# Unread products placed in TensorE's expected stands, in a kernel whose instruction order is planned

## The chip, the cores and the metric

The kernel runs on one core of one Trainium2 chip. The metric is the device time of one execution in microseconds (us); smaller is better. Several executions are measured and the median counts. One execution is also recorded by the hardware profiler, and every reading below is from that one.

## What is computed

Eight sequences `x` of 512 tokens and 256 features go through two layers with residual sums, all in fp32:

```python
x = x + 0.5 * _L0_ffn_ref(_layernorm(x, axis=-1), L0_ffn_w_gate, L0_ffn_w_up, L0_ffn_w_down)
x = x + _L0_attn_ref(_layernorm(x, axis=-1), L0_attn_Wv, ..., L0_attn_Wo)
x = x + 0.5 * _L0_ffn_ref(_layernorm(x, axis=-1), L0_ffn_w_gate, L0_ffn_w_up, L0_ffn_w_down)
x = x + 0.5 * _L1_ffn_ref(_layernorm(x, axis=-1), L1_ffn_gamma_x, ..., L1_ffn_w2)
x = x + _L1_attn_ref(_layernorm(x, axis=-1), L1_attn_wq, ..., L1_attn_bo)
x = x + 0.5 * _L1_ffn_ref(_layernorm(x, axis=-1), L1_ffn_gamma_x, ..., L1_ffn_w2)
```

`_L0_ffn_ref` is a gated FFN of width 704 whose operands are rounded to FP4 in blocks of 16 (so the activations are rounded at run time). `_L0_attn_ref` is a retention layer with decay 0.99. `_L1_ffn_ref` is a soft mixture: 1,024 slots share one expert of width 1,024, with softmax weights over experts on the way in and over slots on the way out. `_L1_attn_ref` is causal attention of 16 heads with LoRA weights.

## The kernel before

The work of a sequence `b` is a row of stages: FFN, retention, FFN and `dispatch` of the mixture (the list `front`, line 1481), then attention and a second `dispatch` (`back`, line 1491). Each `dispatch` is followed by `experts` (line 1055), so there are 16 expert units. Three lanes (`front`, `back`, `experts`, line 1502) each walk through their own list, so that a product of one lane can stand between those of another. A stage is a Python generator that yields ahead of each step which PSUM banks the step takes and which results it needs.

Nothing is ordered by a fixed loop. `drive` (line 1432) chooses the next step by the planned clocks that `Meter` keeps: every instruction of every engine goes through `Meter.emit` (line 139), which estimates when it begins (`begins`, line 125: the latest of its engine's clock, of its inputs' writing and of the last use of its output, plus a hop of 0.12 us between engines) and what it costs (`cost`, line 196), moves that engine's clock and issues it. A step is ready when its needs lie within 0.3 us of TensorE's planned clock; among ready lanes the one that has had least of TensorE goes first. VectorE's small steps (rounding to FP4, normalising, softmax transposes) lie in chains that `fill` and `put_off` put where VectorE is expected to wait. The engines then run their own instructions strictly in that order.

The planner also keeps a model of TensorE's clock (`slow`, line 178). Planned time is cut into stretches of 3.413 us; a stretch with less than 5% of work is followed by half speed, one with more than 90% by full speed, and a stretch between leaves the speed as it is. All of TensorE's instructions count as work there, transposes too.

```python
            if self.worked < 0.05 * self.STRETCH:
                self.full = False
            elif self.worked > 0.9 * self.STRETCH:
                self.full = True
```

Names used below: `gu_f` is the FFN's up and gate product, `dn_f` its down product; `tr_f`, `tr_r` and `tr_m` are transposes of normalised rows ahead of FFN, retention and mixture, `hTp_f` those of the FFN's hidden rows, `nm_m` those of the largest logits; `k_r` and `q_r` are retention's key and query products; `lt_m`, `sl_m`, `h_e`, `p_e` and `mo_e` are the mixture's logits, slots, expert layers and output; `st_a` and `s_a` are attention scores. `y_ffn` is an input row tile, normalised and then rounded in place, `scale_*` and `rec_*` the 16 or 44 block scales of such a tile, `h_f` the hidden rows. `ident` and `identb` (lines 364 to 368) are identity matrices in fp32 and bf16, there for the transposes.

Of the kernel before, what the change touches and what calls it, by code (L numbers as in the profile page):

```python
# [20 lines left out]
FP = mybir.dt.float32  # L21
BF = mybir.dt.bfloat16
# [47 lines left out]
class Meter:  # L70
# [10 lines left out]
    STRETCH = 3.413  # L81
    HOLE = 0.3

    def __init__(self, nc):
        self._nc = nc
        self.at = dict.fromkeys(("PE", "DVE", "ACT", "POOL", "SP"), 0.0)
        self._written, self._used = {}, {}
        self._table, self._mode = None, None
        self.end, self.last = 0.0, None
        self.moved = 0.0  # L90

        self.far = set()

        self.stretch, self.worked, self.full = self.STRETCH, 0.0, False

        self.banks = set()

        self.holds = {"DVE": [], "POOL": []}

        self.kept, self.fill = None, None  # L100
        self.tensor = _Engine(self, "PE", nc.tensor)
        self.vector = _Engine(self, "DVE", nc.vector)
        self.scalar = _Engine(self, "ACT", nc.scalar)
        self.gpsimd = _Engine(self, "POOL", nc.gpsimd)
        self.sync = _Engine(self, "SP", nc.sync)
# [33 lines left out]
    def emit(self, engine, op, call, args, kwargs):  # L139
        aps = [x for x in (*args, *kwargs.values()) if isinstance(x, bass.AP)]  # L140
        if engine == "DVE" and self.fill:

            while self.begins(engine, aps) > self.at[engine] + self.HOLE and self.fill():
                pass
        at, cost = self.begins(engine, aps), self.cost(engine, op, args, kwargs, aps)
        if self.shares(engine, op, aps):

            other = self.holds["POOL" if engine == "DVE" else "DVE"]
            for a, b in sorted(other):
                if a < at + cost and at < b:  # L150
                    at = b
            other[:] = [x for x in other if x[1] > at - 20.0]
            self.holds[engine].append((at, at + cost))
        cost *= self.slow(at, cost) if engine == "PE" else 1.0
        at += cost
        self.at[engine] = self.end = at
        self.last = engine
        if engine == "SP":

            runs = int(np.prod(aps[1].shape[:-1])) if aps[1].ap[-1][0] == 1 else int(np.prod(aps[1].shape))  # L160
            bytes_ = int(np.prod(aps[0].shape)) * 4
            self.moved = max(self.moved, at) + max(bytes_ / self.BYTES, runs * self.RUN)
            self.end = at = self.moved + self.LANDS
        for k in self._pieces(aps[0]):
            self._written[k] = (engine, at)
        for x in aps:
            for k in self._pieces(x):
                self._used[k] = (engine, at)
            self._used[x.tensor.name] = at
        call(*args, **kwargs)  # L170

    def shares(self, engine, op, aps):
        if engine == "DVE":
            ins = sum(x.tensor.name not in self.banks for x in aps[1:])
            return ins > 1 or (op == "tensor_scalar" and self.banks.isdisjoint(x.tensor.name for x in aps))
        return engine == "POOL" and len(aps) > 1
# [104 lines left out]
def macaron(ctx: ExitStack, tc: tile.TileContext, a: dict, out: bass.AP):  # L281
    nc = Meter(tc.nc)
# [81 lines left out]
    ident = const.tile([P, P], FP, tag="ident", name="ident")  # L364
    make_identity(tc.nc, ident)

    identb = const.tile([P, P], BF, tag="identb", name="identb")
    nc.vector.tensor_copy(identb, ident)

    causalb = const.tile([P, 2, P], BF, tag="causalb", name="causalb")  # L370
    causalT = const.tile([P, P], FP, tag="causalT", name="causalT")
# [9 lines left out]
    for u in range(2):  # L381
        t = const.tile([P, NT, P], FP, tag=f"nmx{u}", name=f"nmx{u}")
# [1049 lines left out]
    def drive(until=lambda: False):  # L1432
        while not until():
# [19 lines left out]
            if ready:  # L1453
                emit(min(ready, key=lambda lane: lane.spent))
                continue
# [9 lines left out]
            if found and not (able and first <= nc.at["DVE"]):  # L1465
                go(*found)
            else:
                assert able, [(lane.name, lane.banks, lane.needs) for lane in live]
                emit(min(able, key=lambda lane: when[lane.name]))
# [94 lines left out]
```

## Time and profile before

| | |
|---|---|
| Time, median of 3 executions | 2965.66 us (2959.52 to 2970.26) |
| Profiled execution | 2961.62 us, of which the span from first to last instruction is 2959.7 us |
| TensorE (PE) busy | 2812.0 us, 95% of the span |
| VectorE (DVE), ScalarE (ACT), GpSimd (POOL) busy | 1651.6, 1174.8 and 128.1 us |
| Mean granted TensorE clock | 0.984 |
| PE busy in the first 330 us | 248.6 us, clock 0.89 |
| PE busy from 330 us to 2959 us | 2563.4 of 2629 us |

How to read it: the profile lists for each engine the busy time, and for each product a record of its beginning and modelled end, which overlap a little where products follow one another. "PEclk" is the share of TensorE's full clock that the chip granted. "Idle before" is the time an engine stood ahead of an instruction, with the instruction that released it. All operations are issued from one line of `Meter.emit`, so groups are told apart by the tiles' names. An fp32 product in the code appears as two matmul records.

### The profile page before, as it was taken

Reading aid. Unit: us, or ns where it says so; the run is one execution under the profiler, and the core shown is the slowest. Engines: PE = TensorE matmul, PEld = TensorE weight load, DVE = VectorE, ACT = ScalarE, POOL = GpSimd, SP = SyncE. Lnnn points to the kernel's source line nnn. Section 1 sums busy time; section 2 is a strip of 40 time slices with the busy share of each in tenths; the row PEclk is TensorE's granted clock in tenths of the full one; section 3 lists DMA queues with packets and bytes.
Section 4 is the critical chain, followed back from the end, with each engine's and each line's share of the span. In section 5 each row is a group of like instructions: output and inputs, shape, how many; then the busy total and the mean of one; then the engine's idle time right before and its main releaser. Section 6 shows DMA issues by size and latency. Waiting matters only on the chain.

```text
span 2959.7 us, 35020 instructions
## 1 busy us (share of the span) xinstructions
PE 2812.0 (95%) x13550; PEld 1946.7 (66%) x13550; DVE 1651.6 (56%) x4023; ACT 1174.8 (40%) x1587; POOL 128.1 (4%) x232
## 2 busy tenths in 40 slices
PE   4887999999999999999999999999899999999999
PEld 3554777657676577666766667666577666676668
DVE  7676755566565564655647456555565645436340
ACT  3333443434435343343525425254253443443321
POOL 1000000000000000000000000000000000000000
PEclk8988999999999999999999999999999999999999
DMA  3001101020200220002200031000220012000120
GB/s 118 1 0 35 40 24 45 1 75 1 68 1 1 82 64 5 1 1 82 68 1 1 1 114 36 1 1 1 82 68 1 1 43 79 22 1 20 56 75 8
DMA packets 71335, 98.13 MB, mean 33 GB/s; under 512 B 9472, under 2 KB 56320, under 8 KB 71168
## 3 DMA queue, kind: packets, MB, share of 16 engines
q1 hardware_dynamic: 71168, 95.88, 10.8%
q8 instruction: 107, 1.75, 0.2%
q14 instruction: 60, 0.49, 0.1%
HBM read 58.01 MB, written 37.85 MB: 32 GB/s over the span
## 4 chain that ended last, share of the span: by engine, by line
PE 87%; DVE 6%; ACT 4%; issue 1%; DMA 1%; SPq 1%; POOL 0%; ACTq 0%; DVEq 0%; POOLq 0%
PE p_e L170 14%; PE h_e L170 14%; PE gu_f L170 10%; PE lt_m L170 8%; PE sl_m L170 7%; PE mo_e L170 7%; PE dn_f L170 6%; PE s_a L170 4%; PE st_a L170 3%; PE c_a L170 2%; PE qk_a L170 2%; ACT L170 1%; PE hTp_f L170 1%; PE a_r L170 1%; PE y_r L170 1%; PE k_r L170 1%
## 5 line engine op out<-in xcount | busy, mean ns | idle before, releaser
L170 PE MATMUL h_e<-slT_m,w1g 128*128 128x256 f32 x2048 | 464.9, 381 | 4.2 <-DVE lg_m L170 2.4
L170 PE MATMUL p_e<-w,hid_e 128*128 128x256 f32 x2048 | 456.1, 381 | 3.4 <-ACT hid_e L170 2.0
L170 PEld LDWEIGHTS p_e<-w,hid_e 128*128 128x128 f32 x2048 | 386.3, 190 | 70.6 <-issue 13.3
L170 PEld LDWEIGHTS h_e<-slT_m,w1g 128*128 128x128 f32 x2048 | 382.3, 190 | 74.6 <-issue 11.2
L170 ACT ACT_TABLE_LOAD x274 | 351.5, 1283 | 109.0 <-DVE st_a L170 41.3
L170 PE MATMUL gu_f<-w_in,y_ffn 128*128 128x352 f32 x1024 | 333.8, 478 | 13.3 <-ACT y_ffn L170 11.8
L170 PEld LDWEIGHTS gu_f<-w_in,y_ffn 128*128 128x128 f32 x1024 | 198.7, 197 | 131.3 <-issue 19.4
L170 DVE TENSOR_REDUCE nmx<-s_a 128x2 f32<-128x256 f32 (+3 forms) x256 | 195.9, 818 | 126.3 <-PE s_a L170 126.1
L170 ACT ACTIVATE pT_a<-st_a 128x1024 f32<-128x1024 f32 (+1 forms) x192 | 159.0, 878 | 217.9 <-DVE st_a L170 205.1
L170 PE MATMUL lt_m<-yT_m,seT 128*128 128x512 f32 x512 | 235.5, 607 | 4.1 <-ACT yT_m L170 3.6
L170 ACT ACTIVATE hid_e<-h_e 128x1024 f32<-128x1024 f32 x128 | 130.8, 1023 | 268.5 <-PE h_e L170 268.1
L170 PE MATMUL mo_e<-proc_e,lg_m 128*128 128x257 f32 x1024 | 233.3, 381 | 2.9 <-DVE x L170 1.7
L170 PE MATMUL sl_m<-ed_m,y_dis 128*128 128x512 f32 x512 | 227.1, 594 | 3.9 <-DVE lg_m L170 3.3
L170 PEld LDWEIGHTS mo_e<-proc_e,lg_m 128*128 128x128 f32 x1024 | 190.7, 190 | 39.5 <-issue 4.9
L170 ACT COPY proc_e<-p_e 128x512 f32<-128x512 f32 x64 | 37.5, 586 | 391.9 <-PE p_e L170 391.9
L170 DVE TENSOR_SCALAR_CACHE_REDUCE lg_m<-lt_m 128x512 f32<-128x512 f32 x128 | 84.8, 682 | 173.3 <-PE lt_m L170 173.3
L170 PE MATMUL dn_f<-w_dn,hT_f 128*128 128x256 f32 x768 | 177.3, 383 | 0.0
L170 PEld LDWEIGHTS sl_m<-ed_m,y_dis 128*128 128x128 f32 x512 | 95.9, 190 | 114.9 <-issue 106.7
L170 PEld LDWEIGHTS lt_m<-yT_m,seT 128*128 128x128 f32 x512 | 96.2, 194 | 114.4 <-issue 101.3
L170 DVE TENSOR_TENSOR h_f<-h_f,gu_f 128x352 f32<-128x352 f32 x128 | 66.4, 519 | 177.8 <-ACT h_f L170 177.1
L170 PEld LDWEIGHTS dn_f<-w_dn,hT_f 128*128 128x128 f32 x768 | 143.1, 192 | 23.0 <-issue 4.2
L170 DVE TENSOR_TENSOR st_a<-st_a,causalT 128x256 f32<-128x256 f32 x256 | 100.9, 428 | 100.4 <-PE st_a L170 97.7
(197 smaller groups left out, 3246.3 us busy)
## 6 DMA issues: line engine op xcount, KB each, us to landing
d_ed_m<-ed_m SPq DMA_DIRECT2D x256, 128.0 KB
ed_m<-d_ed_m SPq DMA_DIRECT2D x64, 512.0 KB
rb_m<-row_rb_m SPq DMA_DIRECT2D x32, 256.0 KB
x<-in_L_attn_x SPq DMA_DIRECT2D x8, 512.0 KB
tm_m<-row_nm_m SPq DMA_DIRECT2D x16, 256.0 KB
out<-x SPq DMA_DIRECT2D x8, 512.0 KB
row_rb_m<-z_rb_m SPq DMA_DIRECT2D x128, 0.5 KB
w1g<-in_L_ffn_w SPq DMA_DIRECT2D x1, 1024.0 KB
```

What stands on the lines that cost most here:

```text
L170: call(*args, **kwargs)
```

## The change

`Meter.emit` gets one more step ahead of each TensorE instruction. If the planner expects TensorE to stand for more than `PACE` = 2.2 us ahead of a transpose or the first product of a sum (full height of 128 rows), it looks at which engine writes the awaited input last. From that engine's last 61 outputs (VectorE or ScalarE only, not PSUM) it takes those that are still the latest content of their tile, are two-dimensional with 128 rows and at least 16 contiguous columns, and are expected during the stand, at least 0.5 us ahead of its end. At steps of at most 2.2 us it emits a product of an identity with such an output, of up to 128 columns in fp32 or 512 in bf16 (two of them if it has under 128 columns), into the bank that the awaited product is going to overwrite. Nobody reads the result. These products go through `emit` as well: the planner charges them to TensorE's clock and counts them as work in `slow`.

```diff
+    PACE = 2.2
...
+        self.wrote = {"DVE": [], "ACT": []}
+        self.idents = {}
...
             while self.begins(engine, aps) > self.at[engine] + self.HOLE and self.fill():
                 pass
+        if engine == "PE" and self.idents:
+            self.keep_pace(op, aps, kwargs)
         at, cost = self.begins(engine, aps), self.cost(engine, op, args, kwargs, aps)
...
         for k in self._pieces(aps[0]):
             self._written[k] = (engine, at)
+        if engine in self.wrote and aps[0].tensor.name not in self.banks:
+            self.wrote[engine] = self.wrote[engine][-60:] + [(at, aps[0])]
...
+    def keep_pace(self, op, aps, kwargs):
+
+
+        begin, to = self.begins("PE", aps), aps[0]
+        if begin - self.at["PE"] <= self.PACE or to.shape[0] < 128 or len(to.shape) != 2:
+            return
+        if op != "transpose" and not kwargs.get("start"):
+            return
+        last = [(t + self.HOP, who) for x in aps[1:] for who, t in [self._written.get(k, ("PE", 0.0)) for k in self._pieces(x)]]
+        who = max(last)[1]
+        bank = max((self._used.get(k, ("PE", 0.0))[1] for k in self._pieces(to)), default=0.0) + self.HOP
+        found = []
+        for t, x in self.wrote.get(who, ()):
+            whole = all(self._written.get(k) == (who, t) for k in self._pieces(x))
+            plain = len(x.shape) == 2 and x.shape[0] == 128 and x.shape[1] >= 16 and x.ap[-1][0] == 1
+            if whole and plain and x.dtype in self.idents:
+                found.append((t + self.HOP, x))
+        while begin - self.at["PE"] > self.PACE:
+            now = self.at["PE"]
+            later = [f for f in found if f[0] > max(now + 0.3, bank) and f[0] < begin - 0.5]
+            if not later:
+                break
+            within = [f for f in later if f[0] <= now + self.PACE]
+            x = max(within, key=lambda f: f[0])[1] if within else min(later, key=lambda f: f[0])[1]
+            n = min(x.shape[1], to.shape[1], 512 if x.dtype == BF else 128)
+            for _ in range(1 if n >= 128 else 2):
+                kw = dict(start=True, stop=True)
+                self.run_on("PE", "matmul", (to[:, :n], self.idents[x.dtype], x[:, :n]), kw)
+
+    def run_on(self, engine, op, args, kwargs):
+        idents, self.idents = self.idents, {}
+        self.emit(engine, op, getattr(self._nc.tensor, op), args, kwargs)
+        self.idents = idents
...
     identb = const.tile([P, P], BF, tag="identb", name="identb")
     nc.vector.tensor_copy(identb, ident)
+    nc.idents = {FP: ident, BF: identb}
```

## The prediction, made before the changed kernel was run

> **What bounds the kernel now.** I read the page first: the busy times and the row of granted clocks.
>
> ```profile
> span 2959.7 us, 35020 instructions
> ...
> PE 2812.0 (95%) x13550; PEld 1946.7 (66%) x13550; DVE 1651.6 (56%) x4023; ACT 1174.8 (40%) x1587; POOL 128.1 (4%) x232
> ...
> PEclk8988999999999999999999999999999999999999
> ```
>
> TensorE is the bound. It stands 147.7 us in all (2959.7 - 2812.0), of which the first 330 us hold 81 (330 - 248.6). There the clock is 0.89. Second, the waits of PE, longest total first (total, times, longest):
>
> ```profile
> PE tr_f L170 <- DVE scale_h_f L170: 17.7, 2, 13.9
> PE gut L170 <- DMA Wk<-in_L_attn_Wk: 13.7, 1, 13.7
> PE tr_m L170 <- DVE y_dis L170: 11.9, 4, 3.8
> PE gu_f L170 <- ACT y_ffn L170: 11.8, 14, 3.3
> PE tr_f L170 <- DVE y_ffn L170: 11.3, 2, 6.8
> ```
>
> Few waits are long. Third, the busy time by stretches, cut at 46.95 us + k x 3.413 us. With these cuts every row shows a clock of exactly 1.00 or 0.50, so the clock changes on a fixed grid of 3.41 us (columns: PE, PEld, DVE, ACT, POOL busy, then PEclk):
>
> ```profile
> 67.43:70.84 3.41, 0.56 (x2) 0.00 (x0) 1.18 (x6) 0.00 (x0) 2.94 (x2) 1.00 0.00 0
> 70.84:74.25 3.41, 2.78 (x9) 2.01 (x10) 3.23 (x7) 3.35 (x9) 0.00 (x0) 0.50 0.00 0
> 77.67:81.08 3.41, 2.33 (x14) 1.48 (x13) 2.16 (x5) 2.29 (x5) 0.00 (x0) 1.00 0.00 0
> 81.08:84.49 3.41, 3.41 (x13) 2.24 (x12) 2.39 (x8) 1.14 (x2) 0.00 (x0) 1.00 0.00 0
> ...
> 279.05:282.47 3.42, 0.51 (x2) 0.00 (x0) 2.39 (x6) 3.37 (x7) 0.00 (x0) 1.00 0.00 0
> 282.47:285.88 3.41, 0.00 (x0) 0.00 (x0) 2.74 (x9) 3.40 (x7) 0.00 (x0) 0.50 0.02 5
> ...
> 2869.75:2873.16 3.41, 1.58 (x4) 0.87 (x5) 2.91 (x3) 1.51 (x2) 0.00 (x0) 1.00 0.95 356
> 2873.16:2876.57 3.41, 3.41 (x9) 1.52 (x8) 1.72 (x2) 3.23 (x4) 0.00 (x0) 1.00 0.90 327
> ```
>
> Each pair is a thinly used stretch and the next one. Products (not transposes) for 0.56 us (16%) or 0.51 us (15%) did not keep the clock; 1.58 us (46%) did, and so did the stretch from 77.67 us, with 0.86 us of products and the rest transposes. Fourth, the timeline of PE, for what a lowered clock costs:
>
> ```profile
> 159.08 0.66 PE L170 MATMUL tr_f<-ident,y_ffn 128*128 128x128 f32 x2 [6.75 <-DVE y_ffn L170]
> 160.24 8.04 PE L170 MATMUL gu_f<-w_in,y_ffn 128*128 128x352 f32 x16 [0.51 <-ACT y_ffn L170]
> ...
> 170.16 5.00 PE L170 MATMUL gu_f<-w_in,y_ffn 128*128 128x352 f32 x16 [1.66 <-ACT y_ffn L170]
> ```
>
> The same 16 records take 8.04 us after a stand of 6.75 us and 5.00 us otherwise.
>
> **What the clock costs.** From the stretches and the timeline there are eleven lowered periods ahead of the end. The excess of each is the row at half clock minus the same work elsewhere at full clock. Preceded by one stand over 2.2 us: from 53.8 us (`dnt`, `lora` and half a `gu_f`, about 6 us), 70.8 (`se` 2.52 - 1.04, `gu_f` 4.46 - 2.53: 3.4), 91.3 (`gu_f` 6.69 - 5.00: 1.7), 156.2 (8.04 - 5.00: 3.0), 282.5 (7.41 - 5.00: 2.4), 756.9 (`dn_f` 4.13 - 2.76, `hTp_f` 1.20 - 0.82: 1.8). Sum 18.3 us; call these reachable. Not reachable: from 118.6 (`k_r` 6.32 - 3.60: 2.7), 197.1 (`k_r` 6.65 - 3.60: 3.1), 248.3 (`lt_m` 9.99 - 7.03: 3.0), 989.1 (1.8) and 2084.7 (`lt_m` 5.62 - 3.60 and transposes: 2.6), 13.2 us. Ahead of these the stretch holds several stands of 0.4 to 2.2 us between transposes; none passes `PACE`, and the planner counts the transposes as work. So even a perfect change leaves 13 us. All the reachable work but part of the first period is on the chain that ended last, so a gain there would reach the end.
>
> **What is added.** Nothing is removed or moved by hand; no DMA is added, and no queue is passed.
>
> The trace shows 16 stands of about 2.2 us or more, 80.3 us together, two of them (13.7 and 6.4 us) for weights by DMA. I take the planner's stands to be like these, since its costs are near the rows (0.43 us for a 256-column fp32 product, against two records 0.216 us apart: 32 in 6.91 us in `h_e`). One place per 2.2 us is then at most 36, and some 30 where an output is to be had.
>
> *The price of one.* The trace shows no plain 128-column fp32 product. Half a 256-column one is 0.216 us, 0.43 at half clock. The floor is a small one: 16 or 44 columns, twice, whose array time is less than half of that. Most end in the stand, since the output must come 0.5 us ahead of the awaited one, from the same engine in the same order: a dummy never waits longer than the product behind it. What hides them is the stand. If the stand isn't there (TensorE late against the plan), each costs its 0.216 us: 36 x 0.216 = 7.8 us at full clock. I take a third of 30 on the path at 0.43 us: +4 us (bounds 0 and 8).
>
> *The new waits.* A dummy waits on PE for VectorE or ScalarE, and behind it stands the awaited product. The reverse one is also new: the next writing of the read tile waits for the dummy. The tiles are rewritten much later or are block scales, and TensorE has stood by then. Nothing near in the trace shows such a wait; the hop in the plan is 0.12 us, 30 of them would be 3.6 us if all lay on VectorE's chain, and no gain can come of a wait. I take 0.
>
> *The clock kept.* Here a rule and the rows part. The Trainium skill (TensorE: Matmul & The Clock Gate, section "Why this matters for your kernels") says to leave no idle gap over about 3 us between bursts, since one idle window of about 3.4 us halves the clock. By it a product every 2.2 us breaks every idle window, and all 18.3 us come back. The rows say that a stretch need not be idle: 15 and 16% of use were not enough. A stretch of 3.41 us at a pace of 2.2 us gets one or two dummies, 0.22 or 0.43 us: 6 to 13%, less than what failed. Only with a remainder of other products can they pass: 67.43 us would have 0.56 + 0.22 = 0.78 us (23%), between the failed 16% and the sufficient 46%; I give it half of 3.4 us. The stretch ahead of 91.3 us would have 0.35 + 0.22 = 0.57 us (17%) beside transposes, and gets a third of 1.7. The stretches after 152.8, 282.5 and 753.5 us have no products of their own; together one tenth of 7.2. Ahead of 53.8 us only 44-column scales are about: nothing. Sum 1.7 + 0.6 + 0.7 = 3 us. By the rows, -3; by the rule, -18. The measured rows decide. They leave a gap: records end by a model (some 0.16 us late at the end of a group), so the failed shares may be nearer 10%, and two dummies in one stretch may then do.
>
> *The order.* The dummies enter the plan: it counts them as 6% of a stretch, over its 5%, and so believes in full speed after a stand where it believed in half. From the first such stand its clocks differ by up to 3 us, and all later choices of lanes may fall otherwise. What is at stake is the standing after 330 us, 2629 - 2563.4 = 65.6 us, with single holes such as the 10 us around 2090 us that may vanish or appear. I take 0 as the likeliest and +-12 us as spread.
>
> Sum for the profiled execution: 2961.6 (span 2959.7 plus 1.9 around it) + 4 - 3 = 2962.6. The median of the runs is 4.0 above the profiled one (2965.66 - 2961.62), so 2967.
>
> **Rivals.** *Thin dummies* (45%, the forecast): the clock falls where it fell; 2967, own range 2955 to 2979.
>
> *The clock is kept* (20%): the skill's rule holds, or the true share needed is under 12%. 2965.7 - 18.3 + 4 = 2951, reordering aside. For it: `gu_f` at 8.04 against 5.00 us is real and on the path. Against: the two failed stretches.
>
> *The plan is misled* (35%, slower). One mechanism: the planner prices `gu_f` after a stand at 5.0 us where the chip takes 8.0, and sets behind it steps that it thinks ready; TensorE, in order, stands for one whose input is late, with other lanes' products queued behind. Place: after the six reachable stands and what is ordered from there on. Price: up to 3 us each, 18 us, so 2985. It decides once PE's standing after 330 us grows from 66 to over 75 us. For it: every stand over 2.2 us is a place where the old plan had expected a slow clock. Against: at 120.1 and 198.0 us `k_r` ran 3 us longer than a plan that counts transposes can know, and the next long stand came only at 152 us, and after 198 us only one of 0.28 us by 208.
>
> *It does nothing* (within the first): the outputs found are too narrow or no stand is expected; 2966.
>
> **How the numbers follow.** A measurement of this kernel tells about 0.3% (9 us) from no change. The first case gives 28 points within 9 us, 7 faster, 10 slower; the second 16 faster, 4 within; the third 30 slower, 5 within. Faster 23, same 37, slower 40. The range takes the first case whole and reaches to 2945 (the second case less half the order's spread) and 2992 (the third plus as much).
>
> **What would show it.** Thin dummies: new records with `ident` and an SBUF output, about 30 times 0.22 us; the period from 156.2 us lowered as before and its `gu_f` still near 8 us; mean clock at most 0.988. Kept: mean clock over 0.99 and `gu_f` after stands at 5 us. Misled: the waits of PE after 330 us grow by 9 us or more, at places that have none now. I am wrong if many more than 36 dummies are there, or if they stand behind busy products, with PE's busy time up by over 8 us.

## The result and the profile after

The changed kernel takes 3003.36 us, the median of 4 executions (2997.8 to 3004.84), against 2963.19 us for the kernel before, measured beside it on the same chip. The ratio is 1.0129 (95% interval 1.0116 to 1.0141): 1.3% slower, 36 us above the forecast and 11 us above the top of its range. The profiled execution took 3002.88 us. Its page gives the span, PE's busy time and the row of granted clocks:

```profile
span 3001.0 us, 35150 instructions
...
PE 2848.4 (95%) x13614; PEld 1967.3 (66%) x13614; DVE 1653.7 (55%) x4023; ACT 1182.0 (39%) x1593; POOL 125.3 (4%) x232
...
PEclk8889999999999999999999999999999999999999
```

The span grew by 41.3 us. Only 64 product records are new, one, two or four for each of 22 places, yet PE is busy 36.4 us longer and stands 152.6 us instead of 147.7. The mean granted clock is 0.980, not above the 0.984 of before. So the products meant to keep the clock up came with more lowered clock, not less: the twelve lowered periods of before (96.8 us of the span) became twenty-one (120.5 us). The busy time by two stretches of the changed kernel, then the second stretch of before (columns: PE, PEld, DVE, ACT, POOL busy, then the clock):

```profile
0.00:330.00 330.00, 256.01 (x870) 167.68 (x871) 227.33 (x535) 113.59 (x191) 19.97 (x42) 0.88 0.15 44
330.00:3001.00 2671.00, 2592.42 (x12746) 1799.63 (x12744) 1426.37 (x3489) 1068.41 (x1402) 105.31 (x190) 0.99 0.11 31
```

```profile
330.00:2959.70 2629.70, 2563.37 (x12691) 1783.45 (x12689) 1419.23 (x3466) 1062.84 (x1396) 105.23 (x188) 1.00 0.11 32
```

Nearly all the new products lie in the first 330 us, where PE is busy 7.4 us longer than before. But after 330 us, where new products lie in one stand only (near 2100 us), PE is busy 29 us longer and stands 78.6 us (2671 - 2592.4) instead of 66.3 (2629.7 - 2563.4). Some 10 of these 41 us are work that the kernel before had done ahead of 330 us. The rest, three quarters of the loss, lies far from what was added. The waits of PE, longest total first where they changed (total, times, longest):

```profile
PE tr_f L179 <- DVE y_ffn L179: 22.7, 13, 4.5
PE gut L179 <- DVE gu L179: 14.7, 3, 5.0
PE s_a L179 <- DVE qv_a L179: 10.7, 8, 1.8
...
PE st_a L179 <- ACT pT_a L179: 3.8, 2, 2.8
```

The two long waits of before, 13.9 us for `scale_h_f` and 13.7 us for a weight, have left the top of the list. In their place is a wait for `y_ffn` that comes 13 times instead of twice. Some of the 13 are parts of one stand that the new products (called dummies from here on) break up, and each part counts as a wait. The main point is that other steps now meet each other: this is another order.

How far the changed kernel is behind at equal amounts of real TensorE work can be estimated from the two traces' product records (their columns summed, those of 32-row or 32-column products at a quarter). By the time in the kernel before it is 9 to 11 us from 187 us to 1480 us, then 15 at 1789, 18 at 1998, 23 at 2315, 34 at 2750, 46 at 2852 and 41 at the end; another way of counting moves single values by up to some 5 us. So about 10 us are lost early, where nearly all the new products are, and about 30 us from 1480 us on, where only one stand holds any. One late stretch, before and then after:

```profile
2760.00:2820.00 60.00, 60.00 (x333) 43.66 (x332) 13.12 (x37) 21.76 (x24) 0.80 (x2) 1.00 0.00 1
```

```profile
2760.00:2820.00 60.00, 52.43 (x298) 24.27 (x297) 39.50 (x94) 21.88 (x37) 0.22 (x2) 0.91 0.30 93
```

Before, PE is busy for the whole 60 us at full clock: 39 us of it are an expert unit's layers (`h_e`, `p_e`), beside the last attention. After, the last attention runs there without any: PE stands 7.6 us, 5.2 of them in waits of `st_a` and `s_a` for the softmax (`pT_a`), and the clock drops to 0.91. The timeline of that place shows one such wait:

```profile
2808.37 0.70 PE L179 MATMUL st_a<-qv_a,kv_a 32*128 32x256 f32 x4
2811.85 0.87 PE L179 MATMUL st_a<-qv_a,kv_a 32*128 32x256 f32 x4 [2.77 <-ACT pT_a L179]
```

### The profile page after: what moved, and what is told of

It is laid out like the page before. It is cut to its first block, busy times and chain, and to the rows that moved or that the text cites. A ratio compares the mean times of both kernels' runs of the same rounds, so it can differ in the third digit from the quotient of the medians.

```text
span 3001.0 us, 35150 instructions
## 1 busy us (share of the span) xinstructions
PE 2848.4 (95%) x13614; PEld 1967.3 (66%) x13614; DVE 1653.7 (55%) x4023; ACT 1182.0 (39%) x1593; POOL 125.3 (4%) x232
## 4 chain that ended last, share of the span: by engine, by line
PE 85%; DVE 8%; ACT 4%; issue 1%; DMA 0%; SPq 0%; POOL 0%; ACTq 0%; DVEq 0%; POOLq 0%
PE p_e L179 14%; PE h_e L179 13%; PE gu_f L179 9%; PE lt_m L179 8%; PE mo_e L179 7%; PE sl_m L179 7%; PE dn_f L179 6%; PE s_a L179 4%; PE st_a L179 3%; PE c_a L179 2%; PE hTp_f L179 1%; DVE h_f L179 1%; PE qk_a L179 1%; PE y_r L179 1%; PE a_r L179 1%
## 5 line engine op out<-in xcount | busy, mean ns | idle before, releaser
L179 PE MATMUL sl_m<-ed_m,y_dis 128*128 128x512 f32 x512 | 234.2, 606 | 6.9 <-DVE slT_m L179 6.3
L179 ACT COPY proc_e<-p_e 128x512 f32<-128x512 f32 x64 | 37.6, 587 | 395.0 <-PE p_e L179 395.0
```

## The experiments

**Theories.** *The order*: the credit that the dummies get as "work" in `slow` makes the planner choose other steps, and that order is itself worse. *Misled* (the rival of the prediction): the same credit, but harmful because the chip does not grant the clock that the plan believes in; were it granted, the order would be good. *The products themselves*: their time on PE, or the waits they bring.

### Taking the change apart

`plan_only` plans and credits the dummies but does not issue them; `no_credit` issues them and charges their time, but `slow` doesn't count them as work.

```diff
 # plan_only, in run_on
-        self.emit(engine, op, getattr(self._nc.tensor, op), args, kwargs)
+        self.emit(engine, op, lambda *a, **k: None, args, kwargs)
 # no_credit: counts is 0.0 while run_on emits, else 1.0
-            self.worked += cost * times
+            self.worked += cost * times * self.counts
```

> The changed kernel's plan with every unread product charged and credited in it, but none of them issued: the instructions of the kernel before in the changed kernel's order. Theory 'order' (the new order makes the 40 us): 2985 to 3003 us, at most some 10 us under the changed kernel's 3003. Theory 'products' (the unread products and their waits make it): 2958 to 2970 us, like before.

> The unread products issued and charged to TensorE in the plan, but not counted as work in the planner's clock model; all engines then have the order of the kernel before, with the unread products between. Theory 'order': 2960 to 2973 us, the products' own few us. Theory 'products': 2990 to 3005 us. In both the clock falls at the places of before, since a stretch of 3.41 us gets 6 to 13% of work.

Measured: `plan_only` 3001.8 us, ratio to before 1.0126 (1.0109 to 1.0143); `no_credit` 2964.21 us, 0.9994 (0.9987 to 1.0002). All of the loss is there without a single product added, and none of it with the products alone. In the built programs, `plan_only` has the order of the changed kernel on every engine (but for the dummies), and `no_credit` has the order of before. So the products cost nothing that can be measured, and the line of `slow` that counts them costs it all. (`no_credit` has 30 dummies, the changed kernel 33, since another order has other stands. In the changed kernel's own order the products cost nothing either: its ratio is 1.0129, that of `plan_only` 1.0126.) The page of `plan_only`:

```profile
span 3000.3 us, 35019 instructions
...
PE 2833.6 (94%) x13550; PEld 1955.3 (65%) x13550; DVE 1653.5 (55%) x4023; ACT 1181.6 (39%) x1593; POOL 124.9 (4%) x232
```

It makes the sum plain, since the records are as many as before. Of 40.6 us more span, 19.0 are standing (2959.7 - 2812.0 = 147.7 before, 3000.3 - 2833.6 = 166.7 here). PE's records inside lowered periods add up to 104.3 us instead of 67.0, and half of such time is lost, since the same record takes twice as long there (0.43 us against 0.216): 18.6 us. Together 37.6 of 40.6. In the changed kernel itself the dummies lie in stands: 14.8 us of busy time more than here, and 14.1 us less standing.

The timeline of PE in `no_credit` shows what the products do for the clock:

```profile
152.76 0.94 PE L180 MATMUL tr_f<-scale_x_f,ident 128*128 128x16 f32 x4 [1.97 <-DVE scale_x_f L180]
154.77 1.03 PE L180 MATMUL tr_f<-scale_x_f,ident 128*128 128x16 f32 x4 [1.07 <-DVE scale_x_f L180]
156.51 0.69 PE L180 MATMUL tr_f<-ident,y_ffn 128*128 128x128 f32 x2 [0.71 <-DVE y_ffn L180]
157.70 2.71 PE L180 MATMUL gu_f<-w_in,y_ffn 128*128 128x352 f32 x4 [0.51 <-ACT y_ffn L180]
```

Here three places break the stand that was 6.75 us long before (the first, of two records at 150.30 us, is not shown), none of the pieces is over 2 us, and the `gu_f` behind it still runs slowly: 2.71 us for its first 4 records, 7.67 us for all 16. The clock fell at 152.89 us, ahead of nearly all the narrow products, and they did not bring it back. In the changed kernel the `gu_f` behind such a stand runs slowly too:

```profile
162.81 0.46 PE L179 MATMUL tr_f<-y_ffn,ident 128*128 128x128 f32 x2 [4.46 <-DVE y_ffn L179]
164.08 1.03 PE L179 MATMUL tr_f<-rec_x_f,ident 128*128 128x16 f32 x4 [0.81 <-DVE rec_x_f L179]
165.57 1.04 PE L179 MATMUL tr_f<-rec_x_f,ident 128*128 128x16 f32 x4 [0.46 <-DVE rec_x_f L179]
...
168.01 7.83 PE L179 MATMUL gu_f<-w_in,y_ffn 128*128 128x352 f32 x16 [0.51 <-ACT y_ffn L179]
```

A record with `ident` last is a dummy, one with `ident` first a transpose. This second stand shows less than the first: the input of its first dummy came late, so that a piece of 4.46 us stayed whole, and the clock had fallen at 163.51 us, before the later dummies.

### Granting the clock

If the plan is only misled, then an order made for a full clock must be good once the clock is full. `fill` keeps the order of before and fills each planned stand over 2.2 us with products of the identity with itself, until 0.8 us ahead of its end; the planner's state is put back afterwards, so it knows nothing of them. `after_fill` has the same products under the changed kernel's plan, whose dummies are planned and credited but not issued.

```diff
 # fill
+        state = self.state()
...
+        self.at["PE"] = max(self.at["PE"], bank)
+        while self.at["PE"] < begin - 0.8:
+            self.run_on("PE", "matmul", (to[:, :n], ident, ident[:, :n]), dict(start=True, stop=True))
...
+        self.back_to(state)
 # after_fill: the same, then the dummies of the change with a call that issues nothing
```

> The order of the kernel before; each expected stand over 2.2 us is filled up to 0.8 us ahead of its end with products of the identity with itself, which wait for no output. If a kept clock is worth what the timeline says: up to 18 us less than before at the six reachable places, so 2945 to 2955 us, the mean clock up from 0.984 to 0.990 or more. If the fills end late and delay the awaited products: 2965 to 2980 us. It tells whether the clock can be kept at all and what that is worth.

> The changed kernel's plan and order, but the stands filled as in the run 'fill' in place of the thin products. Theory 'the plan is misled' (the new order is bad because the plan counts on a full clock that the chip doesn't grant): with the clock really kept the order fits, 2945 to 2965 us. Theory 'the order is worse for itself': 2980 to 3000 us, the changed kernel's time less what the kept clock saves, 5 to 15 us.

Measured: `fill` 2942.91 us, 0.9929 (0.9914 to 0.9944), clock 0.997; `after_fill` 2980.07 us, 1.0053 (1.0038 to 1.0068), clock 0.992. The timeline of `fill` at the stand shown above:

```profile
143.88 8.20 PE L179 MATMUL tr_f<-ident 128*128 128x128 f32 x72
151.92 0.38 PE L179 MATMUL tr_f<-ident,y_ffn 128*128 128x128 f32 x2
152.81 5.00 PE L179 MATMUL gu_f<-w_in,y_ffn 128*128 128x352 f32 x16 [0.51 <-ACT y_ffn L179]
```

A stand that is really full keeps the clock here, and `gu_f` takes 5.00 us. This is worth 22 us in either order (about 2965 to 2943, 3002 to 2980). The 18.3 us that the prediction called reachable were thus nearly right in size; what was missing in the change was the amount of work at the right time, not the idea. But the order still costs 37 us with the clock kept in the early stands, so *misled*, as the prediction had it, is not the main cause. The busy time by stretches after 330 us, of `fill` and then of `after_fill`:

```profile
330.00:2942.00 2612.00, 2562.17 (x12803) 1789.36 (x12801) 1412.42 (x3451) 1050.60 (x1382) 105.24 (x188) 1.00 0.11 32
```

```profile
330.00:2981.00 2651.00, 2580.78 (x12777) 1793.92 (x12775) 1416.25 (x3458) 1062.73 (x1394) 103.65 (x188) 0.99 0.10 32
```

Ahead of 330 us both are busy 310.9 us; the whole difference lies behind. Standing is 70.2 us against 49.8, +20.4. Records inside lowered periods are 26.0 us against none, +13.0. These new periods, from 514.6, 914.0, 1931.2, 2453.4, 2760.6 and 2791.3 us, lie mostly at attention's small products with nothing beside them, where no stand was filled. Five of the six stretches ahead of them hold 23 to 53% of work by records, far over the planner's 5%, so its model has no reason to lower the clock there. In this wider sense a wrong clock model may share in the loss, by up to 13 of the 37 us, at places where no dummy stands. Whether a plan with a better bound would avoid them was not tried.

### Is the order bad, or only different?

Other constants of the planner draw other orders too. Each of these has `fill`'s products and one constant changed (two in `fill_b40_h25`); `fill_planned` tells the plan of them (charged and credited); `fill_b40_h25` was chosen because the planner's own end for it is 36 us later than that of before. `hole25` is the kernel before with that constant alone.

```diff
-    HOLE = 0.3
+    HOLE = 0.25
 # fill_slack35: SLACK 0.3 -> 0.35; fill_behind70: BEHIND 60 -> 70
 # fill_b40_h25: BEHIND 60 -> 40 and HOLE 0.25
 # fill_planned: without state() and back_to() around the products
```

> The run 'fill' with one constant of the planner moved by a hair (a step counts as ready within 0.35 us in place of 0.30), which changes the order from the 2,181st TensorE instruction on. Compare with 'fill' (2943 us). Theory 'any other order is worse, that of before is a rare good one': 2960 to 2985 us. Theory 'orders scatter about, and the changed kernel drew a bad one': 2925 to 2965 us, either side of 2943.

> The run 'fill' with the second lane set off by 70 in place of 60 us of planned TensorE time; the order differs from the 191st TensorE instruction on, as early as in the changed kernel. Theory 'any other order is worse': 2960 to 2985 us. Theory 'orders scatter': 2925 to 2965. If the plan's own end tells good orders from bad (it falls by 31 us here, and rose by 11 us for the changed kernel): 2910 to 2920 us.

> The run 'fill' with VectorE's gaps filled from 0.25 in place of 0.30 us on; the order differs from the 137th TensorE instruction on. Theory 'any other order is worse': 2960 to 2985 us. Theory 'orders scatter': 2925 to 2965. If the plan's own end tells (28 us earlier here): 2912 to 2922 us.

> The kernel before with one constant of the planner moved (VectorE's gaps filled from 0.25 in place of 0.30 us on), no product added. If order and kept clock add up, this is 'fill_hole25' (2926 us) without the 22 us that filling gave in the order of before: 2943 to 2953 us, faster than before by the order alone. If the gain of fill_hole25 needs the filled stands: 2960 to 2985 us.

> The filled stands charged and credited in the plan, so that the plan's clock model and the chip agree (in 'fill' they were issued beside the plan). The order is a new one. Theory 'the plan is misled' says that a plan that is right gives a good order: 2915 to 2935 us. Theory 'orders scatter': anywhere in 2925 to 2980 us; the plan's own end (18 us earlier than that of before) says about 2925 to 2935.

> The run 'fill' with two constants of the planner moved (second lane set off by 40 us, VectorE's gaps filled from 0.25 us on), chosen because the plan's own end is 36 us later than that of before. If the plan's own end tells good orders from bad: 2970 to 2990 us. If it tells nothing: 2925 to 2965 us.

| kernel | planner's own end, us | measured, us | ratio to before (interval) |
|---|---|---|---|
| `fill` | 2965.7 | 2942.91 | 0.9929 (0.9914 to 0.9944) |
| `fill_slack35` | 2968.2 | 2950.05 | 0.9957 (0.994 to 0.9973) |
| `fill_behind70` | 2934.6 | 2934.66 | 0.9903 (0.9876 to 0.9931) |
| `fill_hole25` | 2937.7 | 2926.31 | 0.9878 (0.9858 to 0.9898) |
| `hole25`, no products | 2937.7 | 2940.57 | 0.9919 (0.9904 to 0.9933) |
| `fill_planned` | 2947.7 | 2937.6 | 0.9911 (0.9895 to 0.9928) |
| `fill_b40_h25` | 3002.0 | 2980.34 | 1.0052 (1.0037 to 1.0067) |
| `after_fill` | 2976.9 | 2980.07 | 1.0053 (1.0038 to 1.0068) |

The planner's own end is its clock for TensorE when the last instruction has been placed. The four runs with `fill`'s products under other constants, two faster than `fill` and two slower (one chosen for its late end), fit *orders scatter* and not *any other order is worse*; the ends 31 and 28 us earlier had let expect 2910 to 2922 us for `fill_behind70` and `fill_hole25`, and that was not reached. Orders of the same work with the same rule of filling lie between 2926 and 2980 us. A step of 0.05 us in one constant gains as much as filling the clock does (`hole25` against `fill`), and the two add in part: `fill_hole25`, 2926.31 us, is the best version found and beats both kernels, by 1.2% and, 2926.31 against 3003.36 us, by 2.6%. A plan that knows of the filling (`fill_planned`) gains only 5 us over one that doesn't (*misled* had asked for 2915 to 2935 us): right knowledge of the stands is worth little here, and wrong knowledge is therefore no likely price of 37 us by itself. It is one order among many, though, and single orders differ by more than 5 us.

In this table the planner's own end ranks the orders roughly. For the changed kernel it was 2976.9 us, 11 us later than the 2965.7 of before: the planner's own figures said that the new order was worse, although it believed in more clock.

### Where the order loses, and which credits draw it

`after_tail` changes `after_fill` late only: from the planned time of 2200 us the `front` lane counts as having a fifth more of a share, so retention and dispatch go ahead earlier.

```diff
-        lane.spent += (nc.at["PE"] - busy) / SHARE[lane.name]
+        late = 1.2 if lane.name == "front" and busy > 2200.0 else 1.0
+        lane.spent += (nc.at["PE"] - busy) / (SHARE[lane.name] * late)
```

> The run 'after_fill' (2980 us) with the front lane's share raised by 1.2 once the plan has passed 2200 us, so that the seventh sequence's attention, which ended 58 us later there than in 'fill', gets TensorE sooner; the first 5,736 TensorE instructions stay as they are. If the changed kernel's loss lies in its end, where the last two attentions stand with too little expert work beside them: 2950 to 2968 us. If it lies spread over the run: 2975 to 2985 us.

Measured: 2971.26 us, 1.0027 (1.0016 to 1.0037), 9 us less than `after_fill`. The last product of the seventh attention begins at 2647 us in `fill`, 2705 in `after_fill` and 2647 here; the fifteenth mixture's logits at 2671, 2734 and 2669. The seventh attention being 58 us late against `fill` is the likely reason why the last one ran with no expert work beside it. Setting the rank right brought back 9 of 37 us, between the two ranges that had been expected. So the tail looks like one place of the loss, and not most of it; the edit also redraws the order behind it, so the 9 us are not the tail's alone for certain.

Then the credits were given only in part, all else as in `after_fill`: to dummies of stands that end ahead of the planned 60 us, ahead of 170 us, or between 170 and 200 us only. (In the built programs credits ahead of 35 us change no order, and those ahead of 200 us give the changed kernel's order exactly.) Two readings were to be told apart: the credits' harm adds up, or each set simply draws another order.

```diff
 # c_60; c_170: begin < 170.0; c_170_200: 170.0 < begin < 200.0
+        if not begin < 60.0:
+            return
```

> The run 'after_fill' with the thin products' credit in the plan only for stands that end before 60 us of planned time; all stands filled. Theory 'credits add up': between fill (2943) and after_fill (2980) and above fill: 2950 to 2962 us. Theory 'a credit draws another order': the plan's own end is 11 us earlier than that of before, so 2925 to 2945 us.

> As c_60, with the credits up to 170 us of planned time; the order agrees with the changed kernel's up to the 290th TensorE instruction. Theory 'credits add up': 2965 to 2978 us, nearly all of the loss. Theory 'a credit draws another order': the plan's own end is 7 us earlier than that of before: 2928 to 2950 us, and the whole loss comes with the credits of 170 to 200 us that are left out here.

> As c_60, with only the credits from 170 to 200 us of planned time, the ones that turn the order of c_170 into the changed kernel's. Theory 'credits add up': 2946 to 2952 us, a small part. If these credits are bad for any order: 2970 to 2980 us. Theory 'a credit draws another order': bad there need not be bad here; the plan's own end is that of before, so 2935 to 2955 us.

Measured: `c_60` 2951.81 us, 0.9957 (0.9944 to 0.9971); `c_170` 2956.78 us, 0.9973 (0.9964 to 0.9981); `c_170_200` 2955.93 us, 0.997 (0.9962 to 0.9979). Above `fill` these are +9, +14 and +13 us, and all the credits +37. The step from `c_170` to `after_fill` is 23 us for the credits between 170 and 200 us, which alone cost 13. They do not simply add: `c_170` and `c_170_200` fell into neither reading's range. But neither do they scatter to both sides, since all four credited orders are worse than `fill`, while the orders by constants lay at -17, -8, +7 and +37 and `fill_planned` at -5. Four orders that share their credits are too few to settle it. That stays open. These runs also limit the use of the planner's own end: that of `c_60` is 11 us and that of `c_170` 7 us earlier than before's, and yet both are slower than `fill`. An end that counts credits doesn't compare with one that doesn't.

### Thicker products

`thick` keeps the order of before and issues, at each of the change's places, one product of the awaited engine's output and up to four of the identity with itself: more work than the change, less than a full stand.

```diff
+            self.run_on("PE", "matmul", (to[:, :n], self.idents[x.dtype], x[:, :n]), kw)
+            for _ in range(4):
+                if self.at["PE"] < begin - 0.5:
+                    self.run_on("PE", "matmul", (to[:, :m], ident, ident[:, :m]), kw)
```

> The order of the kernel before and the changed kernel's rule of where a product goes, but up to five products of 128 columns at a place (the last four of the identity with itself) in place of one or two: up to 1.1 us of TensorE per 2.2 us, a third of a 3.41 us stretch and more. If the share of a stretch decides whether the clock is kept (between 16 and 46% by the trace of before): most of the gain of 'fill', 2944 to 2954 us, mean clock 0.990 or more. If only an all but gapless TensorE keeps it: 2960 to 2970 us, clock 0.981 to 0.985.

Measured: 2955.35 us, 0.9971 (0.996 to 0.9982), between the two ranges expected; clock 0.984, lowered periods 92 us in all. One stand, ahead of `k_r` at 119.72 us, kept the clock (3.70 us against 6.32 before), but the one shown above, ahead of `gu_f`, did not:

```profile
152.44 1.14 PE L179 MATMUL tr_f<-ident 128*128 128x128 f32 x8
154.71 0.40 PE L179 MATMUL tr_f<-rec_x_f,ident 128*128 128x16 f32 x2 [1.13 <-DVE rec_x_f L179]
154.95 1.77 PE L179 MATMUL tr_f<-ident 128*128 128x128 f32 x8
156.51 0.63 PE L179 MATMUL tr_f<-ident,y_ffn 128*128 128x128 f32 x2
157.65 2.71 PE L179 MATMUL gu_f<-w_in,y_ffn 128*128 128x352 f32 x4 [0.51 <-ACT y_ffn L179]
```

The stretch from 151.86 to 155.28 us is 57% full by records, all of them products, and the next one is lowered: the second group of 8 takes 1.77 us where the first took 1.14. The stretch ahead of it, 65% full with the transposes and 46% without, kept its clock. The record ends are modelled, so the shares are a little high: at `fill`'s spacing (8.20 us / 72 = 0.114 us) the first group occupies 0.91 us and not 1.14.

## Why the prediction was wrong

**The step that failed** is "The order": "I take 0 as the likeliest and +-12 us as spread". The order alone costs 37 us between medians (`plan_only`, 1.0126; +41 us between the profiled executions). The step named the right cause, the 6% of a stretch counted over the planner's 5%, and then gave it no size. It looked at single holes near the stands, where a spread of 12 us seemed ample. What the runs show is that one early credit redraws the whole schedule: the first difference is the 71st TensorE instruction, and three quarters of the places behind it hold another one. The scale of such a redraw could have been learned from the planner itself: its own end moved by +11 us with the change, though it believed in more clock, and over the four neighbouring settings of the table (one chosen as a late one) it runs from 2934.6 to 3002.0 us. Half of the 41 us is standing and half is clock lost in new places; the prediction counted only standing as at stake. Why this order is a bad one, by chance or because such credits favour bad orders, stays open.

**The price of one dummy, the new waits.** Right as far as it can be told: with +4 us for the products, 0 for the waits and -3 us for the clock the sum was +1 us, and `no_credit` is at -2 us (-4 to +1 by its interval). The three parts can't be told apart. The narrow products are not free while the clock is low: four records of 16 columns take 1.03 us, but they lie in the stand.

**The clock kept.** Right that little would come back; even the 3 us of 18.3 were too many. In `no_credit`, with the old order, `gu_f` takes 6.69, 7.67 and 7.31 us at the three stands where it took 6.69, 8.04 and 7.41; at 70.97 us, where half of 3.4 us had been hoped for, the clock fell as before. The account was right only in part. A pace of 2.2 us was planned, but on the chip the outputs came when they came: of the six stands called reachable, five kept a piece of 2.4 to 7.2 us in `no_credit`, two of them (ahead of 90 and 754 us) without any dummy. There the advice to break every gap was not carried out at all.

The Trainium skill (TensorE: Matmul & The Clock Gate, section "Why this matters for your kernels") asks that no idle gap over about 3 us be left. Two stretches decide against taking that as enough: the one from 149.48 us of `no_credit`, whose gaps are at most 1.97 us, and this one of the changed kernel, whose only gaps are one of 1.33 us and one of 2.00 us that runs over its end. PE is busy for half of it, by records, and the next stretch has half the clock:

```profile
50.87:54.28 3.41, 1.71 (x10) 1.28 (x10) 3.27 (x7) 1.09 (x2) 0.00 (x0) 1.00 0.00 0
54.28:57.70 3.42, 1.74 (x8) 1.75 (x9) 3.32 (x6) 0.00 (x0) 0.00 (x0) 0.50 0.02 5
```

A stand that is nearly full kept it (`fill`), one that is 57% full by records did not. The prediction's span of 16 to 46% for the share needed lay too low at its upper end, by these records: products in stands needed more than that.

**The count.** 64 records at 22 places, under the bound of 36; right. (The 16 stands counted for the bound add up to 84.3 us by the trace's records, not 80.3; the bound would be 38.)

**Rival "the clock is kept".** It did not happen in the changed kernel. Its sum was sound: 18.3 us expected, 22 measured in `fill`, which also fills stands ahead of the first lowered period.

**Rival "the plan is misled".** Its test was met: PE's standing after 330 us went from 66.3 to 78.6 us, over the 75 it named. Its forecast of 2985 had the right side. Its mechanism is not what the runs show. The place should have been behind the six stands; there the lag stays at 9 to 11 us until 1480 us. And with the clock granted in the stands, the order still costs 37 us. The test could not tell a misled plan from a worse order, since both grow the standing; it should have named the place as well as the sum.

## What to carry to other kernels

Where a program orders its instructions by a model, an edit to the model is an edit to every instruction behind it: measure "planned but not issued" and "issued but not planned" apart before believing either. Price the redraw from the spread of the planner's own end over a handful of neighbouring settings, all counting the same things, and let that spread, not a zero, stand in the sum. To keep a clock up in a stand, fill it almost whole; here that was worth 22 us, no more than a small step of one planner constant.

## What the runs showed of the hardware beyond that

- Small breaks did not keep the clock: at 150 us of `no_credit` a stand in pieces of at most 1.97 us is followed by half clock from 152.89 us on.
- The share of a stretch that is needed is not one number in the records: 46% of real products (before, from 2869.75 us) and 47% (`thick`, from 165.52 us) kept the clock. Lowered were 42% of real products (`thick`, from 2862.02 us), 53%, all of it attention's products of 32 rows (`after_fill`, from 2757.18 us), 57% of mostly identity products (`thick`, from 151.86 us) and 81% with mostly products of 16 rows (`fill`, from 55.77 us). What makes the difference, the rows in use, the operands or the modelled ends of the records, no run here separates.
- A narrow fp32 product takes as long as a wider one: records of 16 columns follow each other after 0.11 us at full clock (`no_credit`, at 37 us) and 0.21 us at half clock (at 153 us), and those of 128 columns also after 0.11 us (`fill`: 8.20 us / 72).
- The clock's record begins with its first change, at 46.95 us in the kernel before. Ahead of that the profile counts it as 1.00, though `gu_f` took 7.75 us at 41.37 us. So the mean clocks given here leave the first stretch out.
- Filling cost nothing: 852 more records in `fill` than before (14402 against 13550), 61 us more busy time, and a span 18 us shorter.
